# Last layer of a graph network: the gathers' schedule is set to end earlier, and the last bias is added to rows of x one step sooner

## The chip, the cores and the metric

The kernel runs on one core of one Trainium2 chip. The metric is the device time of one execution in microseconds (us), the median of several runs. Less is better.

## The reference

A graph network with 6250 nodes of 256 features, 100000 edges (src, dst; sorted by dst) and four layers:

```python
h = jnp.maximum(_layernorm(x, axis=-1), 0.0)
# three layers:
h = h + segment_sum(h[src], dst)          # each node: itself and its neighbours
h = relu(h @ W1 + b1); h = relu(h @ W2 + b2); h = h @ W3 + b3      # all 256 wide
# fourth and last layer:
h = h + segment_sum(h[src], dst)
h = relu(h @ cW1 + cb1)                   # 256 -> 256
h = relu(h @ cW2 + cb2)                   # 256 -> 64
out = x + (h @ cW3 + cb3)                 # 64 -> 256, and x is added
```

## The kernel before, in words

The nodes lie in 49 blocks of 128. 25 of them are taken as they come ("u"), and 24 hold the other nodes sorted by their number of edges ("s"). Each layer's W1 is multiplied in ahead, so that a layer begins with the neighbour sums, adds b1, and goes on with W2 and W3.

**The neighbour sums are made in two ways, side by side.** (1) *By product*: a matrix of edge counts, one byte each, lies in DRAM (`mat`). A panel is four destination blocks. For each of the 49 source blocks the bytes come to the chip (`at`), ACT or DVE turns them into numbers that TensorE reads (`a`, L1913 on ACT, L1915 on DVE, every fourth one), and TensorE does four products of 128x512 into `agg` (L1942). One source block is called a **step** here: four products. The last layer has 8 panels, 392 steps. (2) *By gather*: for 17 of the sorted blocks, POOL issues indirect DMAs, each of which fetches one neighbour row for all 128 nodes of a block (`rows`, L1627). 251 of them belong to the last layer. ACT copies the first pair of a block into `sums` (L1659), DVE adds the others (L1663), then the block's own rows (`u`, L1676 and L1677), and TensorE turns `u` (`pt`, L1690). The gathered blocks come in groups of four; the last, block 0, stands alone.

**After the sums**, panels and gathered groups take the same road. In the last layer: `head_second` (L1436, the product with cW2, into `ps`), relu on ACT (L1444), `head_third` (L1482, the product with cW3), and an addition of x to the result (`zz`, L1497, on DVE). Rows of x (`xt`) are loaded by `head_rows` when `head_second` is issued: "u" blocks by SP's queue, "s" blocks by an indirect DMA of POOL (L1459). cb3 (`row`) is added to `xt` on DVE when `head_third` is issued (L1476). Results of "s" blocks leave by indirect DMAs on POOL (L596), others by SP's queue. The last panel and block 0 are in a hurry: their x came long before (`ask_first`), and their last addition is L1502. There are three buffers for `zz`, two of PSUM for `ps`, eleven pairs of `rows`, and four for `xt`.

**What sets the order.** All this is written out by a planner while the program is built. A step counts `now` up by one; a clock in estimated us grows with every product. `later(n, f)` writes f's instructions n steps on, and `job` and `queue` do so in a span of steps. For a layer's gathers `begin` sets a pace: from nine units after the layer before has been stored to `CLOSE` (2) units ahead of the layer's end, in equal parts. `flow` and `send` write the gathers by this pace, and each is made to wait for the product that stood last in the program when it was written; `advance` writes the additions and turns of `pair`, `whole` and `finish` by the same pace. A group's W2 and W3 steps follow its turn by fixed distances (`far`, 7 steps; 5 for the last group of four). Each engine takes its own instructions strictly in the order written.

Of the kernel before, what the change touches and what calls it, by code (L numbers as in the profile page):

```python
# [16 lines left out]
OP = mybir.AluOpType  # L17
PSUM = bass.MemoryType.PSUM
DRAM = bass.MemoryType.DRAM
P = 128  # L20
# [400 lines left out]
def sorted_edges(  # L421
# [39 lines left out]
    nc = tc.nc  # L461
    N, C = x.shape
    (E,) = src.shape
    NLAYER = W1s.shape[0]
# [32 lines left out]
    early = [(0, 3)] + [(b, 4) for b in range(3, 27, 4)] + [(27, 3)]  # L497
# [58 lines left out]
    def rows_io(ap, t0, n, sb, load):  # L556

        whole = n if t0 + n < NT or LAST == P else n - 1
        got = []
        if whole:  # L560
            d = ap[t0 * P:(t0 + whole) * P, :].rearrange("(t p) c -> p t c", p=P)
            s = sb[:, :whole, :]
            got.append(nc.sync.dma_start(out=s if load else d, in_=d if load else s))
        if whole < n:
            for r0, r1 in ((0, LAST // 16 * 16), (LAST // 16 * 16, LAST)):
                d = ap[(t0 + whole) * P + r0:(t0 + whole) * P + r1, :]
                s = sb[r0:r1, whole, :]
                got.append(nc.sync.dma_start(out=s if load else d, in_=d if load else s))
        return got
# [12 lines left out]
    def wrote(key, ins, scattered=False):  # L582

        for name, alone in written.setdefault(key, []):
            if scattered or alone:
                tc.declare_no_dep(ins.ins, name, reason="each row is written once")
        written[key].append((ins.ins.name, scattered))
# [3 lines left out]
    def place_rows(key, ap, b, sb):  # L591

        if placing[0]:
            nc.gpsimd.memset(mark, 0.0)
        placing[0] = True
        got = nc.gpsimd.indirect_dma_start(  # L596
            out=ap, out_offset=bass.IndirectOffsetOnAxis(ap=ids[:, b:b + 1], axis=0),
            in_=sb, in_offset=None)
        wrote(key, got, True)
# [72 lines left out]
    def after(ins, reason, what=None):  # L672

        what = paced if what is None else what
        if what:
            tc.add_manual_dep(
                ins.ins, what[0],
                mybir.DependencyInfo(mybir.DependencyClass.Sync,
                                     mybir.DependencyReason.DATA),
                reason=reason,  # L680
            )
# [419 lines left out]
    with tc.manual_schedule():  # L1101
# [52 lines left out]
        weights = {}  # L1154
# [144 lines left out]
        due, jobs, now, free = [], [], [0], [0]  # L1299

        def later(n, fn):
            due.append((now[0] + n, fn))
# [5 lines left out]
        queue = []  # L1308
# [92 lines left out]
        def mlp(l, blocks, h1, hurry, far):  # L1401
# [5 lines left out]
            h2, xts = [], []  # L1407
            key = f"table{l + 1}"

            def runs_of(i, m):  # L1410

                part = [(i + q, 1, *blocks[i + q]) for q in range(m)]
                if m == 2 and part[0][2] == "u" and part[1][2:] == ("u", part[0][3] + 1):
                    return [(i, 2, "u", part[0][3])]
                return part
# [34 lines left out]
            def head_rows():  # L1450
                if hurry:
                    return
                for o, f, m in ((0, 0, front), (NOUT, front, n - front)):
                    if not m:
                        continue
                    xt = late.tile([P, 2, C], F32, name="xt", bufs=4)
                    for i, k, kind, b in runs_of(f, m):
                        if kind == "s":
                            got = nc.gpsimd.indirect_dma_start(  # L1459
                                out=xt[:, i - f, :], out_offset=None, in_=x[:, :],  # L1460
                                in_offset=bass.IndirectOffsetOnAxis(ap=ids[:, b:b + 1], axis=0))
                            after(got, "rows are asked for evenly over a layer")
                        else:
                            if b + k == NT and LAST < P:
                                nc.vector.memset(xt[:, i - f + k - 1, :], 0.0)
                            rows_io(x, b, k, xt[:, i - f:i - f + k, :], True)
                    xts.append(xt)

            def head_third():
                w3, row = weights[l][1]  # L1470
                sets = [(o, f, m) for o, f, m in ((0, 0, front), (NOUT, front, n - front)) if m]
                pss = []
                for k, (o, f, m) in enumerate(sets):
                    if not hurry:
                        xt = xts[k]
                        nc.vector.tensor_tensor(xt[:, :m, :], xt[:, :m, :],  # L1476
                                                row[:, None, :].to_broadcast([P, m, C]), OP.add)
                    pss.append(ps_m.tile([P, W], F32, name="ps"))
                for q in range(front):
                    for (o, f, m), ps in zip(sets, pss):  # L1480
                        if q < m:
                            mm = nc.tensor.matmul(ps[:, q * C:(q + 1) * C],  # L1482
                                                  h2[0][o:o + NOUT, 0, q * P:(q + 1) * P],
                                                  w3[o:o + NOUT, :], start=True, stop=True)
                    passed(C * FULL32, mm)

                def give(f, m, z):
                    for i, k, kind, b in runs_of(f, m):
                        if kind == "s":
                            place_rows("out", out[:, :], b, z[:, i - f, :])  # L1490
                        else:
                            for got in rows_io(out, b, k, z[:, i - f:i - f + k, :], False):
                                wrote("out", got)

                def ended(f, m, ps, z, xt):
                    if not hurry:
                        nc.vector.tensor_tensor(z[:, :m, :],  # L1497
                                                ps[:, :m * C].rearrange("p (q c) -> p q c", c=C),
                                                xt[:, :m, :], OP.add)
                        return  # L1500
                    for q in range(m):
                        nc.vector.tensor_tensor(z[:, q, :], ps[:, q * C:(q + 1) * C],  # L1502
                                                first_x[blocks[f + q]][:, 0, :], OP.add)

                for k, ((o, f, m), ps) in enumerate(zip(sets, pss)):
                    z = work.tile([P, 2, C], F32, name="zz", bufs=3)
                    xt = None if hurry else xts[k]
                    later(soon, lambda f=f, m=m, ps=ps, z=z, xt=xt: ended(f, m, ps, z, xt))
                    later(soon + 1, lambda f=f, m=m, z=z: give(f, m, z))
# [56 lines left out]
            def thirds():  # L1566
                passed(BURST)
                if end:
                    head_third()
                    return  # L1570
                for i in range(0, n, 2):
                    third(i)

            wait = 1 if hurry else far - 2
            queue.append(dict(steps=[seconds, thirds], first=now[0] + wait,
                              last=now[0] + wait + (0 if hurry else SPAN),
                              far=2 if hurry else far, hurry=hurry))


        class ByNode:  # L1580
# [21 lines left out]

            def begin(self):
                self.first = clock[0] + LAG
                self.pace = (begun[self.l] + work_of(self.l) - CLOSE - self.first) / len(self.order)

            def flow(self):
                if self.first is not None:
# [254 lines left out]
        last = [len(panels[l]) - 1 for l in range(NLAYER + 1)]  # L1863
        units = [(0, -1, j) for j in range(PRE)] + [
            (l, p, j) for l in range(NLAYER + 1) for p in range(last[l] + 1) for j in range(NT)]
        LAG, CLOSE = 9.0, 2.0
        COLS, FULL32, TURN, BUILD, SLOW, BURST = 0.457e-3, 1.68e-3, 0.4, 0.25, 1.0, 0.3
        clock = [0.0]
        FAR, SPAN = 7, 6
# [5 lines left out]
        def work_of(l):  # L1875

            t = sum(n for _, n in panels[l]) * P * NT * 2 * KC * COLS
            t += len(layers[l].blocks) * TURN
            for k, n in ((l, NT - panels[l][-1][1]), (l - 1, panels[l - 1][-1][1])):
                t += (k >= 0) * n * (P * KC + C) / 2 * (1 if k == NLAYER else 4) * FULL32  # L1880
            t += 2 * (len(nodes_of[l]) + last[l]) * BURST
            if l == 0:
                t += BUILD * UNITS * BUILT + PRE * (SLOW - BUILD)
            return t

        def passed(t, ins=None):

            clock[0] += t
            if ins is not None:
                paced[:] = [ins.ins.name]  # L1890
                for g in layers:
                    g.flow()
# [85 lines left out]
        with tc.tile_pool(name="hots", bufs=1) as hots, tc.tile_pool(  # L1978
# [6 lines left out]
            begun = {0: clock[0]}  # L1985
# [94 lines left out]
```

## Time and profile before

| | |
|---|---|
| runs | 2000.32, 2002.68, 2003.56 us; median 2002.68 us |
| the profiled execution | 1999.98 us, its span 1998.2 us |
| granted TensorE clock, mean | 0.976 |
| last layer's 392 steps | the last products end at 1981.5 us of the span |
| from there to the end of the span | 16.7 us |

Times in the rows are us from the start of the span. A row of the timeline gives start, duration, engine, line, operation and count, and in brackets how long the engine stood idle before it and what released it. The chain of waits is followed back from the last instruction; its rows give start, duration and what ran. In the view by stretches each engine has its busy time and, in brackets, its number of instructions; PEclk is the granted clock of TensorE, 1.00 being full speed.

### The profile page before, as it was taken

What the parts mean: (1) busy time and instruction counts of PE and PEld (TensorE: products, weight loads), DVE (VectorE), ACT (ScalarE), POOL (GpSimd) and SP (SyncE); (2) the same over time, 40 slices, a digit from 0 to 9 for tenths busy, and PEclk for the clock granted to TensorE, in tenths of its full rate; (3) what the DMA queues carried; (4) which work ended last, traced back from release to release, by engine and by line L of the source; (5) the groups of instructions that cost most, each with busy time, mean ns of one, the idle gap of its engine ahead of it and who ended that gap; (6) DMA issues with size and microseconds to landing.
All of it is one profiled execution on the core that took longest, in us unless ns stands there. A gap on an engine that the chain in (4) does not pass through costs nothing.

```text
span 1998.2 us, 29053 instructions
## 1 busy us (share of the span) xinstructions
PE 1883.4 (94%) x9236; PEld 1471.0 (74%) x9236; DVE 1030.9 (52%) x2211; ACT 1075.0 (54%) x2166; POOL 1309.6 (66%) x1447
## 2 busy tenths in 40 slices
PE   5856999999999899999999999999999999999997
PEld 3744777777777777777789777777788777777765
DVE  7887887676756343333335443433345354343433
ACT  4745776676767564444445464444445564454442
POOL 2526766766666556777777476676777366777775
PEclk9876999999999999999999999999999999999998
DMA  5524656666656575565557575564657476665653
GB/s 167 177 75 141 202 182 191 199 199 200 208 171 215 160 233 162 173 183 168 181 179 210 160 247 175 154 194 146 196 165 236 147 217 200 186 197 175 181 175 109
DMA packets 252334, 361.40 MB, mean 181 GB/s; under 512 B 33353, under 2 KB 206313, under 8 KB 252155
## 3 DMA queue, kind: packets, MB, share of 16 engines
q1 hardware_dynamic: 188160, 190.34, 30.2%
q0 software_dynamic: 61952, 166.87, 28.0%
q10 hardware_dynamic: 2058, 2.25, 0.4%
q8 instruction: 74, 1.21, 0.2%
q14 instruction: 90, 0.73, 0.1%
HBM read 292.33 MB, written 67.40 MB: 180 GB/s over the span
## 4 chain that ended last, share of the span: by engine, by line
PE 82%; DVE 7%; DMA 5%; issue 3%; POOL 2%; ACT 1%; SPq 0%; DVEq 0%; ACTq 0%; POOLq 0%
PE agg L1942 64%; PE ps L1519 6%; PE ps L1422 6%; DMA rows<-table,idxN 3%; PE bp L1259 2%; PE bp L1050 1%; DVE ws L768 1%; DVE hi L1205 1%; POOL rows L1627 1%; PE pt L1690 1%; POOL lane L1748 1%; DVE lo L1205 1%; PE ps L1436 1%; PE ps L1482 0%; ACT a L1913 0%
## 5 line engine op out<-in xcount | busy, mean ns | idle before, releaser
L1942 PE MATMUL agg<-a,XY 128*128 128x512 f32 (+1 forms) x6272 | 1508.8, 392 | 16.0 <-DVE a L1915 7.3
L1627 POOL DMA_INDIRECT rows<-table,idxN x1121 | 1084.5, 967 | 474.6 <-PE agg L1942 202.6
L1942 PEld LDWEIGHTS agg<-a,XY 128*128 128x128 f32 x6272 | 1142.6, 189 | 249.5 <-issue 12.4
L1913 ACT CAST a<-at 128x512 fp32r<-128x512 uint8 (+1 forms) x1249 | 707.3, 601 | 235.0 <-PE agg L1942 225.7
L1663 DVE TENSOR_TENSOR sums<-sums,rows 128x512 f32<-128x512 f32 x477 | 331.7, 695 | 502.2 <-DMA rows<-table,idxN 461.3
L1915 DVE CAST a<-at 128x512 fp32r<-128x512 uint8 (+1 forms) x312 | 142.0, 460 | 166.3 <-PE agg L1942 143.3
L1267 ACT CAST at<-bp 128x392 uint16<-128x392 f32 x227 | 110.0, 488 | 127.2 <-PE bp L1259 122.0
L1422 PE MATMUL ps<-h,w 128*128 128x512 f32 (+2 forms) x336 | 135.0, 545 | 0.3 <-DVE zz L1524 0.3
L1519 PE MATMUL ps<-w,h 128*128 128x256 f32 x588 | 133.9, 379 | 0.0
L1205 DVE TENSOR_TENSOR lo<-lanes,pairs 128x512 bf16<-128x512 bf16 x256 | 106.7, 422 | 45.6 <-PE bp L1259 44.9
L1259 PEld LDWEIGHTS <-lo 128*128 128x128 bf16 x1028 | 57.0, 102 | 97.3 <-DVE lo L1205 41.4
L1259 PE MATMUL bp<-hi,lo 128*128 128x98 bf16 x1028 | 94.4, 218 | 34.5 <-DVE lo L1205 27.7
L1519 PEld LDWEIGHTS ps<-w,h 128*128 128x128 f32 x588 | 111.5, 190 | 16.0
L596 POOL DMA_INDIRECT table<-zz,ids x72 | 72.5, 1007 | 68.3 <-DVE zz L1524 49.3
L1659 ACT COPY sums<-rows 128x512 f32<-128x512 f32 x74 | 43.8, 592 | 126.4 <-DMA rows<-table,idxN 91.2
L1425 ACT ACTIVATE h<-ps,bias 128x512 f32<-128x512 f32 (+2 forms) x84 | 51.6, 636 | 96.2 <-PE ps L1422 96.1
L1422 PEld LDWEIGHTS ps<-h,w 128*128 128x128 f32 x336 | 62.9, 192 | 52.8 <-issue 37.6
L1698 ACT ACTIVATE h<-pt,bias 128x256 f32<-128x256 f32 (+1 forms) x84 | 33.0, 444 | 127.7 <-PE pt L1690 127.7
L1524 DVE TENSOR_TENSOR zz<-ps,w 128x512 f32<-128x512 f32 (+1 forms) x81 | 50.5, 638 | 96.6 <-PE ps L1519 83.2
L1349 DVE TENSOR_TENSOR XY<-back,XY 128x256 fp32r<-128x256 f32 x138 | 54.7, 422 | 46.3 <-ACT XY L1348 45.9
L1956 ACT ACTIVATE h<-agg,bias 128x512 f32<-128x512 f32 (+1 forms) x60 | 37.3, 669 | 72.5 <-PE agg L1942 72.3
L1205 DVE TENSOR_TENSOR hi<-hi,pairs 128x784 bf16<-128x784 bf16 x128 | 72.7, 568 | 4.4
(239 smaller groups left out, 957.3 us busy)
## 6 DMA issues: line engine op xcount, KB each, us to landing
at<-mat SPq DMA_DIRECT2D x140, 448.0 KB
mat<-at SPq DMA_DIRECT2D x32, 784.0 KB
at<-mat SPq DMA_DIRECT2D x62, 336.0 KB
rows<-table,idxN POOLq DMA_INDIRECT x1121
back<-table SPq DMA_DIRECT2D x138, 128.0 KB
table<-zz SPq DMA_DIRECT2D x35, 256.0 KB
at<-mat SPq DMA_DIRECT2D x63, 112.0 KB
own<-zz SPq DMA_DIRECT2D x55, 128.0 KB
```

The source lines that it names most:

```text
L596: got = nc.gpsimd.indirect_dma_start(out=ap, out_offset=bass.IndirectOffsetOnAxis(ap=ids[:, b:b + 1], axis=0), in_=sb, in_offset=None)
L1205: nc.vector.tensor_tensor(o, values, which[:, :, None, :].to_broadcast(shape), op)
L1259: mm = nc.tensor.matmul(bp[:, m * HW:(m + 1) * HW], lo[:, m, :], hi[:, m, :], start=(i == 0), stop=(i == len(sets) - 1))
L1267: nc.scalar.copy(o, v)
L1349: later(1, lambda: nc.vector.tensor_tensor(XY[:, j:j + m, C:], z[:, :m, :], XY[:, j:j + m, :C].bitcast(F32), OP.subtract))
L1422: mm = nc.tensor.matmul(ps[:, :w], weights[l][0][:, c, i * P:(i + 1) * P], h1[:, c, :w], start=(c == 0), stop=(c == KC - 1))
L1519: mm = nc.tensor.matmul(o, h2[0][:, c, nodes], w3[:, c, :], start=(c == 0), stop=(c == KC - 1))
L1627: got = nc.gpsimd.indirect_dma_start(out=t[:, c % 2, :], out_offset=None, in_=tables[self.l][:, :], in_offset=bass.IndirectOffsetOnAxis(ap ...
L1663: nc.vector.tensor_tensor(sums, sums, rows.rearrange("p h c -> p (h c)"), OP.add)
L1913: nc.scalar.copy(o, v)
L1915: nc.vector.tensor_copy(o, v)
L1942: mm = nc.tensor.matmul(agg[c][:, :w], XY[:, j, o:o + P], a[:, :w], start=(i == 0 and half == 0), stop=(i == NT - 1 and half == 1))
```

## The change

Two things change, both in the last layer.

1. In `begin`, the last layer's gathers are laid out to end `4 * CLOSE` (8) units ahead of the layer's end, where it was `CLOSE` (2). The other layers keep 2. The additions and turns that use the gathered rows are written by the same pace and move with them.
2. The addition of cb3 to `xt` leaves `head_third`. It is written by `later(far - 1, ...)` when the rows are asked for, so one step ahead of `head_third`, which comes `far` steps after. What is computed is the same.

```diff
                     xts.append(xt)
+                    later(far - 1, lambda xt=xt, m=m: nc.vector.tensor_tensor(
+                        xt[:, :m, :], xt[:, :m, :],
+                        weights[l][1][1][:, None, :].to_broadcast([P, m, C]), OP.add))
...
             def head_third():
-                w3, row = weights[l][1]
+                w3 = weights[l][1][0]
...
-                for k, (o, f, m) in enumerate(sets):
-                    if not hurry:
-                        xt = xts[k]
-                        nc.vector.tensor_tensor(xt[:, :m, :], xt[:, :m, :],
-                                                row[:, None, :].to_broadcast([P, m, C]), OP.add)
+                for _ in sets:
                     pss.append(ps_m.tile([P, W], F32, name="ps"))
...
             def begin(self):
                 self.first = clock[0] + LAG
-                self.pace = (begun[self.l] + work_of(self.l) - CLOSE - self.first) / len(self.order)
+                early = 4 * CLOSE if self.l == NLAYER else CLOSE
+                self.pace = (begun[self.l] + work_of(self.l) - early - self.first) / len(self.order)
```

The changed file is shorter by one line above the third product, so L1482, L1497 and L1502 read L1481, L1496 and L1501 in it; the bias addition L1476 reads L1468.

**TensorE, about 160 steps from the end of the layer.** `ps` at L1436 is the second product of a gathered group, `agg` the panels' products, `pt` a turn. Before:

```order
L1482 MATMUL ps<-cw_15930,h_17693 128x256 x4
L1942 MATMUL agg<-a,XY 128x512 x32
L1690 MATMUL pt<-ident,u 128x128 x2
L1942 MATMUL agg<-a,XY 128x512 x44
L1436 MATMUL ps<-h_17461,w_15928 64x256 x4
```

and now:

```order
L1481 MATMUL ps<-cw_15930,h_17697 128x256 x4
L1942 MATMUL agg<-a,XY 128x512 x16
L1690 MATMUL pt<-ident,u 128x128 x2
L1942 MATMUL agg<-a,XY 128x512 x44
L1436 MATMUL ps<-h_17439,w_15928 64x256 x4
```

The third product (first row) belongs to a panel and stands at the same step in both, 173 steps ahead of the layer's end. The second product of the gathered group follows 76 products later before and 60 now: 154 and 158 steps ahead of the end, so it moved four steps. Its four gathers of x on POOL moved with it.

**TensorE, the end of the layer.** The `pt` in the first row shown is block 0's, the last one; L1436 of 64x128 and L1482 (now L1481) without a count are block 0's two products, and the last L1436 and L1482 are the last panel's. Before:

```order
L1690 MATMUL pt<-ident,u 128x128 x2
L1942 MATMUL agg<-a,XY 128x512 x12
L1482 MATMUL ps<-cw_15930,h_19340 128x256 x4
L1436 MATMUL ps<-h_19361,w_15928 64x128 x2
L1482 MATMUL ps<-cw_15930,h_19398 128x256
L1436 MATMUL ps<-h_19376,w_15928 64x256 x4
L1482 MATMUL ps<-cw_15930,h_19409 128x256 x4
```

and now:

```order
L1690 MATMUL pt<-ident,u 128x128 x2
L1436 MATMUL ps<-h_18901,w_15928 64x256 x4
L1942 MATMUL agg<-a,XY 128x512 x20
L1481 MATMUL ps<-cw_15930,h_19319 128x256 x4
L1942 MATMUL agg<-a,XY 128x512 x16
L1436 MATMUL ps<-h_19310,w_15928 64x128 x2
L1942 MATMUL agg<-a,XY 128x512 x4
L1481 MATMUL ps<-cw_15930,h_19391 128x256
L1436 MATMUL ps<-h_19399,w_15928 64x256 x4
L1481 MATMUL ps<-cw_15930,h_19409 128x256 x4
```

Block 0's turn stood 12 products (3 steps) ahead of the layer's end and stands 40 (10 steps) ahead now. Behind it and ahead of the end there are now also the last group's second product (L1436, four instructions, which stood ahead of the turn before), its third product (L1481) and block 0's second product, which both came after the last `agg` before.

**DVE, the end of the layer.** `h` at L1953 is half of the last panel's relu, `u` the sums of block 0. Before:

```order
L1677 TENSOR_TENSOR u<-u,sums 128x256
L1953 TENSOR_SCALAR h_19376<-agg,bias 128x512
L1476 TENSOR_TENSOR xt<-xt,cb3r 128x512 x2
L1497 TENSOR_TENSOR zz<-ps,xt 128x512 x2
L1502 TENSOR_TENSOR zz<-ps,back 128x256 x5
```

and now:

```order
L1677 TENSOR_TENSOR u<-u,sums 128x256
L1915 CAST a<-at 128x512
L1468 TENSOR_TENSOR xt<-xt,cb3r 128x512 x2
L1915 CAST a<-at 128x512
L1496 TENSOR_TENSOR zz<-ps,xt 128x512 x2
L1953 TENSOR_SCALAR h_19399<-agg,bias 128x512
L1501 TENSOR_TENSOR zz<-ps,back 128x256 x5
```

The last group's bias additions and its additions of x stood behind the last panel's relu and stand ahead of it now, with casts for the product still to come between them.

More of the change, by code (lines that the diff above doesn't have):

```diff
@@ L1574, in mlp @@
             wait = 1 if hurry else far - 2
-            queue.append(dict(steps=[seconds, thirds], first=now[0] + wait,
-                              last=now[0] + wait + (0 if hurry else SPAN),
-                              far=2 if hurry else far, hurry=hurry))
+            queue.append(dict(
+                steps=[seconds, thirds], first=now[0] + wait,
+                last=now[0] + wait + (0 if hurry else SPAN), far=2 if hurry else far, hurry=hurry))
         class ByNode:
```

## The prediction

> **What bounds the kernel now.** I read the page first, then the chain of waits over the last 120 us, then the timelines of POOL and TensorE there.
>
> ```profile
> PE 1883.4 (94%) x9236; PEld 1471.0 (74%) x9236; DVE 1030.9 (52%) x2211; ACT 1075.0 (54%) x2166; POOL 1309.6 (66%) x1447
> 1717.00:1790.00 73.00, 55.36 (x61) 1.00 0.63 193
> 1790.00:1811.50 21.50, 14.23 (x15) 1.00 0.62 187
> 1811.50:1974.70 163.20, 125.17 (x139) 0.99 0.56 168
> L1627 POOL DMA_INDIRECT rows<-table,idxN x99 | 95.7, 967 | 30.7 <-issue 15.8 <-PE agg L1942 10.9 <-DVE sums L1663 0.9
> 1810.66 0.94 POOL L1627 DMA_INDIRECT rows<-table,idxN  x1 [0.89 <-PE agg L1942]
> 1811.91 0.95 POOL L1459 DMA_INDIRECT xt<-in_x_dram,ids  x1 [0.30 <-PE ps L1436]
> 1973.66 0.94 POOL L1627 DMA_INDIRECT rows<-table,idxN  x1 [0.31 <-issue]
> ```
>
> TensorE is busy for 94% of the span, so over the whole it is the bound. The next three rows are stretches, POOL's busy time behind the length. An indirect DMA costs POOL 0.95 to 0.97 us and a pause of 0.30 even where it waits for nothing, so POOL is full at 0.76 busy. It is full from 1717 to 1790 (55.4 of 73), is not from 1790 to 1811 (14.2 of 21.5), and is full again from 1811 to the last gather at 1973.66 (125.2 of 163.2). The fifth row says the same of the 99 gathers from 1811 on: 30.7 us of idle time ahead of them, 0.31 each. At 1810.66 a gather still waited for TensorE; after it none really did. In the last 160 us POOL is behind, and its own rate decides when rows come.
>
> ```profile
> 1973.66 2.79 DMA rows<-table,idxN
> 1976.58 0.71 DVE sums L1663
> 1977.76 0.43 DVE u L1677
> 1978.33 0.41 PE pt L1690 x2
> 1978.74 2.79 PE agg L1942 x12
> 1982.30 1.29 DVE xt L1476 x2
> 1983.63 0.56 DVE zz L1497
> 1988.36 2.63 DMA out_dram<-zz,ids
> 1991.73 0.41 DVE zz L1502 x2
> ```
>
> The end of the chain of waits (rows of it). The last gather lands, its sums are done, block 0 is turned at 1978.33: 4.67 us from the issue. Twelve products end the layer at 1981.53. I call this point P. Then the bias additions (1.29 us), the additions of x, four scatters of POOL, the landing of the fourth at 1990.99, and the last additions, done at 1992.14. The stores and the end of the program take the 6.06 us to 1998.2.
>
> ```profile
> 1919.39 3.06 PE L1942 MATMUL agg<-a,XY 128*128 128x512 f32 x12 [1.55 <-DVE a L1915]
> 1924.54 2.01 PE L1942 MATMUL agg<-a,XY 128*128 128x512 f32 x4 [2.08 <-ACT a L1913]
> 1978.33 0.41 PE L1690 MATMUL pt<-ident,u 128*128 128x128 f32 x2 [1.38 <-DVE u L1677]
> 1925.50:1926.50 1.00, 1.00 (x4) 0.50 0.47 131
> 1927.50:1928.50 1.00, 1.00 (x4) 0.72 0.54 164
> 1928.50:1930.00 1.50, 1.50 (x8) 1.00 0.87 204
> ```
>
> TensorE stands still for 1.55, 2.08 and 1.38 us in the last panel, each time for gathered rows: directly, or because a cast stands in DVE's or ACT's queue behind an addition that waits for them. After the second wait the granted clock was near half from 1924.5 to 1928.2, as the last three rows show. At half rate 3.7 us cost 1.8 us.
>
> **The change part by part.** No instruction is added or removed: the same gathers, x rows, scatters and SP loads stand in other places.
>
> *When do the gathers end?* The new pace spreads six planner units over 251 gathers. Where POOL waits for TensorE, a gather moves by as many steps as its place in the program; where POOL is full, nothing moves it but the work ahead of it. The full stretch that reaches the end begins with the four gathers of x at 1811.91, which wait for the second product 154 steps ahead of the end. That product now stands at 158. The queue ahead has room: between 1790 and 1811 POOL was idle beyond its pauses by 21.5 - 14.23/0.76 = 2.8 us, and the earlier pace lets it begin that stretch sooner. So POOL starts its last run four steps sooner. It then works off the same instructions, so the last gather is issued four steps sooner.
>
> ```profile
> 1903.52 10.27 PE agg L1942 x44
> 1900.21 1.01 PE ps L1436 x8
> 1913.79 1.06 PE ps L1482 x8
> 1903.30 0.22 PE pt L1690 x2
> ```
>
> Eleven steps take 10.27 us, so a step is 0.934 us, and four are 3.74 us. Bounds: 2.8 us (only the slack between 1790 and 1811) and 5.6 us (all six steps). I take 3.7, since it follows from the place in the program.
>
> *What waits for it?* Block 0's turn moved seven steps, from 3 to 10 ahead of the end, while its last row comes only four steps sooner. So this wait grows. The turn cannot start ahead of 1978.33 - 3.74 = 1974.59. TensorE is there long before: it reached the old place at 1978.33 - 1.38 = 1976.95, and seven steps (6.5) and the last group's second product (1.01) lie behind the turn now, so it would come at 1969.4, plus what the waits in the middle change. The wait at the turn is some 5 us. **This is the step on which the forecast rests.** It also covers whatever else the change does to TensorE in the middle of the panel, up to 5 us either way.
>
> *From the turn to P.* The turn 0.22, the second product 1.01, ten steps 9.34, the third product 1.06, and block 0's second product about 0.31 (half of the row of 0.62 below, which ran slowly): 11.94 us. P would be 1986.5 where it was 1981.53: +5.0. (A trace row counts each fp32 matmul twice: x8 is four instructions.)
>
> *The clock.* 2.08 us of waiting were enough to halve it, so some 5 us are. Cost 1.8 us, as in the row. Bounds: 0 and 3.6 (twice the span). The half rate after the earlier waits was paid before too, and is covered by the wait anyway. +1.8.
>
> *From P to the last addition.*
>
> ```profile
> 1981.16 0.69 ACT L1956 ACTIVATE h<-agg,bias 128x512 f32<-128x512 f32 x1 [1.76 <-PE agg L1942]
> 1984.99 0.36 ACT L1444 ACTIVATE h<-ps,bias 64x128 f32<-64x128 f32 x1 [3.14 <-PE ps L1436]
> 1984.33 0.62 PE L1436 MATMUL ps<-h,w 128*64 128x128 f32 x4 [1.75 <-DVE zz L1497]
> 1985.40 0.70 PE L1482 MATMUL ps<-cw,h 64*128 64x256 f32 x2 [0.45 <-ACT h L1444]
> 1986.03 1.97 PE L1436 MATMUL ps<-h,w 128*64 128x256 f32 x8
> 1988.10 0.47 ACT L1444 ACTIVATE h<-ps,bias 128x256 f32<-128x256 f32 x1 [2.75 <-PE ps L1436]
> 1988.63 2.08 PE L1482 MATMUL ps<-cw,h 64*128 64x256 f32 x8 [0.63 <-ACT h L1444]
> 1990.73 1.42 DVE L1502 TENSOR_TENSOR zz<-ps,back 128x256 f32<-128x256 f32 x4 [4.17 <-PE ps L1482]
> ```
>
> It took 10.6 us, for bias, additions and scatters of the last group stood in it. They stand ahead of P now. What is left, by these rows: ACT's relu ends 0.3 behind P (1981.16 + 0.69); block 0's relu 0.36 and a handover to P + 0.8; its third product and the start of the next, 0.63, to P + 1.4; the second product of the last panel at full clock 1.01, to P + 2.4; relu with handovers 0.63, to P + 3.1; the third product at full clock, of which three quarters are needed for the first addition, 0.9, to P + 4.0; four additions 1.42, to P + 5.4. So 5.2 us are saved. But these two products took 1.97 and 2.08 us before, not 1.01 and 1.06, because the clock had fallen after a gap of 1.75 and one of 0.45 us. The new gaps are a little shorter. I take one of the two products at half rate, +1.0; bounds 0 and +2.0.
>
> [...]
>
> *The bias one step sooner.* 22 additions of x rows move by a step. In the last group this is part of the 5.2. Elsewhere it makes DVE stand for x rows if POOL brings them late, with row additions and casts queued behind. Priced at nothing: what it does to TensorE lies ahead of the turn, under its 5 us.
>
> *Sum.* +5.0 + 1.8 - 5.2 + 1.0 = **+2.6 us** on the profiled 1999.98, and as much on the median of 2002.68: **2005.3 us**. The profiled execution is 2.7 below the median, so runs differ by more than this sum. Bounds: with no clock lost -0.2; with all of it lost +5.4; with the gathers' shift at 2.8 a further +0.9, at 5.6 a further -1.9.
>
> **The rivals.** About 0.2%, 4 us, is what a measurement of this kernel can tell from no change.
>
> *The clock holds* in the tail, or at the turn too: +1.6 or -0.2, 2002.5 to 2004.3. For it: 1.38 us at 1978.33 brought no fall. Against: 1.75 did.
>
> *POOL is held up by DVE, slower.* The place: the middle of the last panel. DVE stands at the bias addition for x rows that POOL has not yet fetched; it frees no row buffers meanwhile; POOL, out of pairs, stops; and every us that it stops is one at the last gather, uncovered. It decides once DVE stands longer than eleven pairs last, 22 gathers at 1.25 us less those under way. Against: of the gathers' idle time only 0.9 us is put down to DVE before. With 4 us lost: +6.6, 2009.3.
>
> *The waits go away, faster.* If rows came in time, the waits of 1.55, 2.08, 1.38 and the 1.8 of clock would go: P at 1981.53 - 6.8 + 1.4 (products moved ahead of it) = 1976.1, the last addition 5.4 later at 1981.5 instead of 1992.1: -10.6, 1992.1. Half of it gives 1997.4. For it: this is the stretch where TensorE waits. Against: POOL has no free slot in the last 160 us.
>
> **How the numbers follow.** The forecast, a longer wait at the last turn paid back by a shorter tail, has 45%, with a range of its own from 2003 to 2008; 15 of these points are above +4 (both tail products slow, a longer fall of the clock). The clock holds: 13%. Slower by POOL: 24%. Faster: 18%. Within 0.2%: 30 + 13 = 43%. Slower: 24 + 15 = 39%. Faster: 18%. The range that leaves two in ten out goes from 1998 to 2010.
>
> **What would show it.** Right: the last gather 3 to 5 us sooner against the start of the last layer; a wait of 4 to 6 us ahead of block 0's turn, with a clock near 0.5 behind it; P some 5 to 7 us later; about 6 us instead of 10.6 from P to the last addition, with no scatter in the chain. Wrong: a wait under 2 us at the turn, POOL idle for TensorE or DVE after 1811, or the last gather no sooner.

## The result and the profile after

| | before | after |
|---|---|---|
| median of 22 runs each, on one chip | 2000.74 us | 2004.94 us |
| ratio after/before | | 1.0013, 95% interval 1.0007 to 1.0019 |
| span of the profiled execution | 1998.2 us | 2003.1 us |
| granted TensorE clock, mean | 0.976 | 0.977 |

By the ratio the change costs 2.6 us (1.4 to 3.8). The medians lie 4.2 us apart and the means of the same runs 3.1: the change is slower by all three, by how much is less sure than the interval says. The two spans differ by more, 4.9 us, but 2.7 of these lie ahead of the last layer, where the change edits nothing. So the last layer is measured from its own start, its first gather. The timeline of POOL has it, in the kernel before:

```profile
1589.38 0.97 POOL L1627 DMA_INDIRECT rows<-table,idxN  x1 [11.54 <-PE agg L1942]
```

and in the changed kernel, with the first gather of x in POOL's last run, the last gather, and the gathers' group from there on:

```profile
1592.10 0.97 POOL L1627 DMA_INDIRECT rows<-table,idxN  x1 [11.72 <-PE agg L1942]
1810.93 0.95 POOL L1459 DMA_INDIRECT xt<-in_x_dram,ids  x1 [0.30 <-PE ps L1436]
1972.47 0.98 POOL L1627 DMA_INDIRECT rows<-table,idxN  x1 [0.30 <-issue]
L1627 POOL DMA_INDIRECT rows<-table,idxN x98 | 94.3, 962 | 29.9 <-issue 14.3 <-PE agg L1942 10.4 <-DMA rows<-table,idxN 1.2
```

Against the layer's start the last gather is issued at 380.37 us; it was 384.28. So it is 3.9 us sooner, and not six steps (5.6 us, the prediction's upper bound). The last row says why: 98 gathers with 29.9 us of idle time ahead of them, 0.31 each, which is POOL's own pause. As before, POOL has nothing to give in the last 160 us; it started this stretch 3.7 us sooner (1810.93 - 1592.10 = 218.83, where it was 222.53) and ended it as much sooner.

TensorE's timeline of the changed kernel, from the middle of the last panel to the end:

```profile
1922.14 3.78 PE L1942 MATMUL agg<-a,XY 128*128 128x512 f32 x8 [5.59 <-DVE a L1915]
1977.06 0.41 PE L1690 MATMUL pt<-ident,u 128*128 128x128 f32 x2 [3.37 <-DVE u L1677]
1978.41 6.47 PE L1942 MATMUL agg<-a,XY 128*128 128x512 f32 x20
1985.88 4.00 PE L1942 MATMUL agg<-a,XY 128*128 128x512 f32 x16
1989.80 0.65 PE L1436 MATMUL ps<-h,w 128*64 128x128 f32 x4
1990.38 1.18 PE L1942 MATMUL agg<-a,XY 128*128 128x512 f32 x4
1992.14 0.70 PE L1481 MATMUL ps<-cw,h 64*128 64x256 f32 x2 [0.57 <-ACT h L1444]
1992.76 1.08 PE L1436 MATMUL ps<-h,w 128*64 128x256 f32 x8
1994.48 1.13 PE L1481 MATMUL ps<-cw,h 64*128 64x256 f32 x8 [0.63 <-ACT h L1444]
```

The waits of 1.55 and 2.08 us in the middle became one of 5.59, and the wait of 1.38 at block 0's turn became 3.37. The last products end at 1991.56 (P). The two products of the tail ran in 1.08 and 1.13 us where they took 1.97 and 2.08. The granted clock (PEclk) behind the turn, by stretches:

```profile
1978.00:1979.00 1.00, 1.00 (x7) 0.53 (x4) 0.69 (x1) 1.00 (x4) 0.67 (x1) 0.70 0.46 131
1979.00:1980.00 1.00, 1.00 (x4) 0.80 (x3) 0.00 (x0) 1.00 (x3) 0.00 (x0) 0.50 0.48 131
1980.00:1982.00 2.00, 2.00 (x7) 1.58 (x6) 1.03 (x2) 0.04 (x1) 0.00 (x0) 0.55 0.00 0
1982.00:1984.00 2.00, 2.00 (x10) 1.61 (x9) 0.00 (x0) 0.00 (x0) 0.00 (x0) 1.00 0.00 0
1991.00:1997.00 6.00, 3.41 (x21) 1.60 (x19) 2.53 (x6) 1.41 (x3) 1.88 (x3) 1.00 0.21 71
```

The shares missing to 1.00 make 0.30 + 0.50 + 0.90 = 1.7 us. The last row is the tail: 1.00 throughout. The chain of waits covers only the last 0.66 us here, with no scatter and no transfer in it (its three rows). What stands ahead of it is in DVE's timeline (last row): the last four additions waited for the third product.

```profile
1996.40 0.20 DVE zz L1501
1996.60 0.05 issue
1996.65 0.41 DVE zz L1501
1995.64 1.42 DVE L1501 TENSOR_TENSOR zz<-ps,back 128x256 f32<-128x256 f32 x4 [2.35 <-PE ps L1481]
```

The last addition ends at 1997.06, 404.96 us after the layer's start, where it was 402.77: **2.2 us later**, near the 2.6 of the ratio. The rest of the span is 6.04 us, where it was 6.05.

### The profile page after: what moved, and what is told of

It reads as the page before. It is cut to its first block, busy times and chain, and to the rows that moved or that the text cites. A ratio compares the mean times of both kernels' runs of the same rounds, so it can differ in the third digit from the quotient of the medians.

```text
span 2003.1 us, 29042 instructions
## 1 busy us (share of the span) xinstructions
PE 1882.5 (94%) x9236; PEld 1470.6 (73%) x9236; DVE 1031.9 (52%) x2211; ACT 1074.8 (54%) x2166; POOL 1311.6 (65%) x1447
```

## The experiments

This table has, for each kernel whose trace is used, the last gather's issue and the end of the last addition in us from the layer's first gather (each against before in brackets), the time from there to the end of the span, and the time against before by the ratio, with its interval. Each kernel has one trace, and not all were taken on one chip; the ratios compare runs of one chip.

| kernel | last gather | last addition | to the end | time against before, us |
|---|---|---|---|---|
| before | 384.28 | 402.77 | 6.05 | |
| the change | 380.37 (-3.9) | 404.96 (+2.2) | 6.04 | +2.6 (+1.4 to +3.8) |
| bias alone | 384.67 (+0.4) | 403.38 (+0.6) | 5.88 | -1.6 (-3.4 to +0.2) |
| pace alone | 381.05 (-3.2) | 405.56 (+2.8) | 6.05 | +2.8 (+1.0 to +4.6) |
| change, wait filled | 380.42 (-3.9) | 403.43 (+0.7) | 5.85 | -1.0 (-2.8 to +0.8) |
| change, x rows by SP | 365.87 (-18.4) | 388.84 (-13.9) | 12.76 | -8.2 (-11.4 to -5.2) |
| bias, gathers ahead | 374.24 (-10.0) | 402.29 (-0.5) | 5.89 | -1.2 (-3.0 to +0.4) |
| the same, x rows asked early | 373.88 (-10.4) | 394.98 (-7.8) | 5.82 | -8.8 (-11.2 to -6.4) |
| the same, pace 6 units | 370.84 (-13.4) | 390.82 (-11.9) | 6.14 | -12.2 (-15.6 to -9.0) |

### The two parts apart

The bias addition moved, the pace as before:

```diff
-                early = 4 * CLOSE if self.l == NLAYER else CLOSE
+                early = CLOSE
```

> The bias part alone; the gathers' pace is that of before. Theory (the change's cost is the wait at block 0's turn, which comes from the pace): the turn stays 3 steps ahead of the end with a wait of about 1.4 us, P does not move, and the 1.29 us of bias additions leave the chain behind P: 1 to 1.5 us faster than before. Rival (the cost is DVE standing at the earlier bias addition for x rows, 6.59 and 1.73 us in the middle of the last panel of the change): slower than before by 1 to 4 us, with those waits of DVE in the trace.

The median was 2001.5 us against 2002.63, ratio 0.9992 (0.9983 to 1.0001). TensorE's timeline, and a row of DVE's:

```profile
1919.84 2.08 PE L1942 MATMUL agg<-a,XY 128*128 128x512 f32 x4 [6.26 <-DVE a L1915]
1980.30 0.41 PE L1690 MATMUL pt<-ident,u 128*128 128x128 f32 x2
1986.10 0.62 PE L1436 MATMUL ps<-h,w 128*64 128x128 f32 x4 [1.54 <-DVE zz L1496]
1988.29 1.97 PE L1436 MATMUL ps<-h,w 128*64 128x256 f32 x8
1990.89 2.08 PE L1481 MATMUL ps<-cw,h 64*128 64x256 f32 x8 [0.63 <-ACT h L1444]
1984.00 0.69 DVE L1468 TENSOR_TENSOR xt<-xt,cb3r 128x512 f32<-128x512 f32 x1 [1.85 <-DMA xt<-in_x_dram,ids]
```

The moved addition does make DVE stand in the middle of the panel: the gap there is 6.26 us. But the turn behind it then waits for nothing (1.4 us were expected), and no loss against before is shown. The last gather did not come later by more than 0.4 us. The rival in which the bias addition holds up POOL falls. The gain of 1 to 1.5 us is not shown either: the ratio's interval holds both it and nothing, and in the trace the last addition comes 0.6 us later. The last row shows why the tail (what follows P) is no shorter: the last group's bias addition still ends behind P, since it waits for x rows that POOL fetches behind the last gather.

The pace alone, with the bias addition in its old place:

```diff
-                self.pace = (begun[self.l] + work_of(self.l) - CLOSE - self.first) / len(self.order)
+                early = 4 * CLOSE if self.l == NLAYER else CLOSE
+                self.pace = (begun[self.l] + work_of(self.l) - early - self.first) / len(self.order)
```

> The pace part alone; the bias stays in the third step. Theory: block 0's turn stands 10 steps ahead of the end and waits 3 to 5 us for its rows, the clock falls to 0.5 behind it, P comes 5 to 7 us later than before against the start of the layer, the tail takes 5.5 to 6 us; 2 to 3.5 us slower than before, as the whole change. Rival (DVE at the bias addition): the gap of TensorE near 1920 shrinks from 5.6 to under 3 us and the time is that of before within 1 us.

2004.67 us against 2002.63, ratio 1.0014 (1.0005 to 1.0023): the whole cost of the change. At the end of the layer TensorE shows the same picture as the whole change, the wait longer, since the middle has shorter gaps than the change (3.02 and 1.18 us):

```profile
1919.38 4.92 PE L1943 MATMUL agg<-a,XY 128*128 128x512 f32 x20 [3.02 <-ACT a L1914]
1972.96 0.66 PE L1691 MATMUL pt<-ident,u 128*128 128x128 f32 x2 [4.08 <-DVE u L1678]
1973.55 1.98 PE L1436 MATMUL ps<-h,w 128*64 128x256 f32 x8
1990.27 1.13 PE L1482 MATMUL ps<-cw,h 64*128 64x256 f32 x8 [0.63 <-ACT h L1444]
```

The waits in the middle are no shorter than before (3.02 and 1.18 us, where 1.55 and 2.08 stood), and the turn waits 4.08 where it waited 1.38. The 3.02 us kept the clock: the 20 products behind them took 4.92 us. The tail is short and at full clock here too, so it is the pace that shortens it, by moving the last group's work ahead of P.

### The clock behind the wait

The change, with 24 transposes that nobody reads written ahead of block 0's turn, so that TensorE works while it waits:

```diff
+                    if self.l == NLAYER and b == 0:
+                        for _ in range(24):
+                            nc.tensor.transpose(self.pt[:, 0, :P], ident, ident)
```

> The change, with 24 needless transpositions of a constant (about 2.6 us of TensorE work, overwritten at once) ahead of block 0's turn, so that TensorE works instead of waiting there. Theory (1.7 us of the loss are the clock behind that wait): the clock stays at 1.00 behind the turn and 1.5 to 1.9 us are won against the change: 0.5 to 1.5 us slower than before. Rival (the clock costs nothing, or the wait is not the bound): 2.5 us slower than before as the change, or 2.6 us more, slower by 5.

2001.2 us, ratio 0.9995 (0.9986 to 1.0004). The filler, the turn, and the products behind it:

```profile
1970.37 2.78 PE L1691 MATMUL pt<-ident 128*128 128x128 f32 x24
1974.35 0.44 PE L1693 MATMUL pt<-ident,u 128*128 128x128 f32 x2 [1.20 <-DVE u L1677]
1975.73 4.93 PE L1945 MATMUL agg<-a,XY 128*128 128x512 f32 x20
```

The 20 products took 4.93 us where they took 6.47, and the last addition comes 1.5 us sooner than in the change. So the half clock after the wait costs what the windows gave, 1.5 to 1.7 us, and by the trace the kernel is 0.7 us slower than before, as expected. By the two ratios the kernel won 3.6 us on the change, with intervals of 1.2 and 1.8 us on either side; more than the profile shows, and not told apart from it.

### Fewer gathers on POOL

The change, with the x rows of sorted blocks loaded by SP's queue. They are taken as they lie in DRAM and not by the sorted list, so other rows of x are added; the bytes are the same.

```diff
-                            got = nc.gpsimd.indirect_dma_start(
-                                out=xt[:, i - f, :], out_offset=None, in_=x[:, :],
-                                in_offset=bass.IndirectOffsetOnAxis(ap=ids[:, b:b + 1], axis=0))
-                            after(got, "rows are asked for evenly over a layer")
+                            rows_io(x, b, 1, xt[:, i - f:i - f + 1, :], True)
```

> The change, with the x rows of sorted blocks loaded by SP's queue from block order instead of POOL's indirect DMAs: wrong rows of x are added there, at the same number of bytes. 18 of POOL's last 132 indirect DMAs go, 22 us of its queue. Theory (POOL's rate sets the last gather): the last gather comes 10 to 20 us sooner, the waits of TensorE in the last panel and at the turn fall under 1 us, and the kernel is 8 to 16 us faster than before. Rival (rows land in time and the waits come from the order on DVE and ACT): the last gather moves, the time stays within 2 us of the change.

1994.84 us, ratio 0.9959 (0.9943 to 0.9974). The last gather comes 18.4 us sooner than before, TensorE has no gap in the last panel, and the turn waits for nothing, though it stands 10 steps ahead of the end as in the change:

```profile
1961.98 0.41 PE L1687 MATMUL pt<-ident,u 128*128 128x128 f32 x2
```

So it is POOL's queue that made rows late. Gathered rows and rows of x both come sooner here; this kernel does not part the two. The last addition comes 13.9 us sooner, and only 8.2 us arrive in the time: the end of the program takes 12.76 us behind it instead of 6. The view of waits has in this kernel

```profile
SPq L2073 <- PEq L2073: 7.6, 2, 7.0
```

and in the changed kernel, for the same wait (us in total, times, longest):

```profile
SPq L2076 <- PEq L2076: 0.7, 2, 0.5
```

SP's queue waits 7.0 us for TensorE's sequencer at the very end, though TensorE's last product ended 14 us before the span does. What its sequencer did there the trace does not show.

### Gathers ahead, consumers in place

The next three kernels give up the change's pace and let each gather of the last layer be sent further ahead of its additions. The first has before's pace, the moved bias addition, and:

```diff
-                    self.send(int((clock[0] - self.first + LAG) / self.pace) + 1)
+                    self.send(int((clock[0] - self.first + (2 * LAG if self.l == NLAYER else LAG)) / self.pace) + 1)
```

The second also asks for the x rows of a group when the group is put in the queue, and not at its second product; the bias addition keeps its step. (In the functions of the changed kernel: `head_rows()` at the end of `mlp`, and the `later(far - 1, ...)` in `seconds`.) The third has 18 units written in place of `2 * LAG`, which is the same number since `LAG` is 9, and lays its gathers out to end `3 * CLOSE` (6 units) ahead of the layer's end: it differs from the second in this pace alone. A fourth kernel is the change with `8 * CLOSE` in place of `4 * CLOSE`.

> The change with its pace taken back (the last layer spreads its gathers over the same time as before) and, in its place, every gather of the last layer sent LAG = 9 more units of work ahead of its additions; the additions, turns and products stay where before has them. Theory (the change loses because its consumers, above all block 0's turn, move further than the last gather does): here the turn stays three steps ahead of the end, so the wait ahead of it must be no longer than the bias-alone kernel's, and the time is not above that of before: -3 to 0 us, with the tail of 5 to 6 us between the end of the products and the last addition less what cold products cost. The gap in the middle of the last panel may grow (vector engine standing at the bias addition for x rows that now queue behind nine units more of gathers), 5 to 8 us, and be covered. Rival (any earlier laying-out of the gathers costs, since POOL then collides with other work): 2 us or more above before. Rival (only the last gather's issue decides): as much faster as the last gather is sooner, 4 to 8 us.

> The change with 8 * CLOSE (16 units) in place of 4 * CLOSE (8). Theory: POOL works off the same instructions at 1.25 us each, and its last run begins with the gathers of x rows, which move with their place in the program; the last gather comes some 8 to 12 us sooner than in before, but block 0's turn moves as far again, so the time stays 1 to 4 us above that of before, and the wait at the turn stays 2 to 5 us. Rival (the plan's intent: gathers that end sooner give a shorter time): 4 us or more below before. Rival (each unit of pace costs more): 5 us or more above before.

> As the kernel that sends the last layer's gathers 9 units further ahead with before's pace and the bias addition early; and the x rows of the last layer are asked for when a group is put in the queue (ahead of its second product by some ten steps) and not at the second product itself, while the bias addition keeps its step. Theory (the waits in the last panel are consumers that come ahead of their rows: DVE at the bias addition, then block 0's turn): both go, no gap above 1.5 us in the last panel, the clock stays at 1.00 to the turn, and the time is 6 to 11 us below before. Rival (POOL's rate alone decides the end, whatever stands where): last gather as in before and within 2 us of before. Rival (the end of the program, which came 12.75 us behind the last addition and not 6.0 in the run with x rows by SP, takes a part back): 2 to 5 us below before, with the span's end 10 us or more behind the last addition.

> As the run before it, with the gathers a fixed 18 units ahead of their place and a pace of 3 * CLOSE (6 units) in the last layer. Theory: the last gather comes some 10 us sooner than in before, nothing waits for it, the last panel runs without a gap, and the time is 3 us or so below the run before it, 9 to 14 us below before. Rival (the program's end takes it back): not below the run before it, with the span's end 10 us or more behind the last addition. Rival (POOL then stands without pairs of row buffers and is held up): the last gather is no sooner than in the run before it and the time is equal or more.

These four first ran on a chip on which the kernel before takes 2176.41 us. In the order of these expectations they gave ratios of 1.0021 (1.0007 to 1.0035), 1.0031 (1.0015 to 1.0047), 1.0033 (1.0016 to 1.0049) and 1.0010 (0.9993 to 1.0027). In the groups of before, on the first chip, TensorE's main products have this idle time ahead of them over the span:

```profile
L1942 PE MATMUL agg<-a,XY 128*128 128x512 f32 (+1 forms) x6272 | 1508.8, 392 | 16.0 <-DVE a L1915 7.3 <-ACT a L1913 3.9 <-DVE a L1911 2.7
```

and in the kernel with x rows asked early, on this chip:

```profile
L1944 PE MATMUL agg<-a,XY 128*128 128x512 f32 (+1 forms) x6272 | 1572.4, 401 | 106.6 <-issue 73.6 <-ACT a L1915 15.8 <-ACT h L1958 6.8
```

"issue" is time in which the engine waited for nothing that the profile shows: 73.6 us of it, summed over the span. There TensorE often stands by itself, and the layer's end is set by that as well as by rows. So none of the expectations, which are sums of waits for rows, is decided by these ratios. Of the kernel with `8 * CLOSE` they say no more than that it isn't faster there (6.7 us above before, 3.3 to 10.2); its turn waits 2.16 us for its rows. It has no run on another chip; the other three have.

> The kernel of the first rows-ahead run once more. In that call the kernel before itself took 2176 us and TensorE's main products stood 73.6 us for nothing that the profile names, in any layer, so nothing was told apart. On a chip where before takes some 2002 us: theory (the waits in the last panel are consumers that come ahead of their rows): no gap above 1.5 us for rows in the last panel, 6 to 11 us below before. Rival (POOL's rate alone decides): within 2 us of before. Rival (the program's end takes a part back): 2 to 5 us below, with 10 us or more from the last addition to the span's end. Where before takes 2176 us again: no difference beyond the interval.

> The second rows-ahead kernel once more (18 units, 3 * CLOSE), for the same reason. Theory: last gather some 10 us sooner than in before, nothing waits for it, 9 to 14 us below before. Rival (the program's end takes it back): not below the first rows-ahead kernel. Rival (POOL stands without row buffers): last gather no sooner than in the first.

> The kernel with before's pace, the bias early and the gathers 9 units further ahead, x rows asked for as in before, once more for the same reason. Theory: its turn stays three steps ahead of the end, so -3 to 0 us against before, with a gap of 5 to 8 us in the middle of the last panel at the bias addition, for the x rows queue behind nine units more of gathers. Rival (any earlier laying-out costs): 2 us or more above before.

On a chip where before takes 2001.91 us they gave, in this order, 1993.53 us, 0.9956 (0.9944 to 0.9968); 1989.74 us, 0.9939 (0.9922 to 0.9955); and 2000.67 us, 0.9994 (0.9985 to 1.0002). The last of these, with the gathers ahead alone, comes first here:

```profile
1915.64 2.08 PE L1942 MATMUL agg<-a,XY 128*128 128x512 f32 x4 [7.46 <-DVE a L1915]
1975.52 0.38 PE L1690 MATMUL pt<-ident,u 128*128 128x128 f32 x2
1981.60 0.62 PE L1436 MATMUL ps<-h,w 128*64 128x128 f32 x4 [1.85 <-DVE zz L1496]
1911.49 0.69 DVE L1468 TENSOR_TENSOR xt<-xt,cb3r 128x512 f32<-128x512 f32 x1 [13.72 <-DMA xt<-in_x_dram,ids]
```

(TensorE's rows and one of DVE's.) Its last gather is **10.0 us sooner** than before, its turn waits for nothing, and yet its last addition is 0.5 us sooner. The gain is lost in the middle: the x rows are now behind nine units more of gathers in POOL's queue, DVE stands 13.72 us at the bias addition, its casts stand behind it, and TensorE stands 7.46 us. The tail has half rate besides, behind a gap of 1.85 us. With the x rows asked early, and the same gathers (last one at -10.4):

```profile
1901.93 1.39 DVE L1557 TENSOR_TENSOR xt<-xt,cb3r 128x512 f32<-128x512 f32 x2 [2.69 <-DMA xt<-in_x_dram,ids]
1945.04 0.69 DVE L1557 TENSOR_TENSOR xt<-xt,cb3r 128x512 f32<-128x512 f32 x1 [9.88 <-DMA xt<-in_x_dram,ids]
1947.46 4.00 PE L1944 MATMUL agg<-a,XY 128*128 128x512 f32 x16 [1.15 <-DVE a L1917]
1970.40 0.38 PE L1692 MATMUL pt<-ident,u 128*128 128x128 f32 x2
1977.06 0.62 PE L1436 MATMUL ps<-h,w 128*64 128x128 f32 x4 [2.41 <-DVE zz L1493]
1978.75 1.08 PE L1436 MATMUL ps<-h,w 128*64 128x256 f32 x8
1984.82 0.76 DVE L1498 TENSOR_TENSOR zz<-ps,back 128x256 f32<-128x256 f32 x2 [2.43 <-PEq L2054]
```

The same addition stands 2.69 us, and the time is 8.8 us below before, 7.6 below the kernel without the early x rows. DVE still stands 9.88 us at the next group's addition, near 1945, but that costs TensorE only 1.15 us, its largest gap in the last 75 us ahead of P: it seems to matter which cast is queued behind, and when TensorE needs it. The two differ in nothing but when the x rows are asked for. Not all of the 7.3 us between their last additions are waits for rows: the tail's two products kept the clock here and did not there, 1.08 and 1.14 us for 1.96 and 2.08, which is 1.8 us. On the other side the last two additions stood 2.43 us for TensorE's sequencer (last row), which no other kernel of the table did; without that the last addition would be 10.2 us sooner than before, and not 7.8.

The third, with the pace of 6 units, has its last gather at -13.4 and takes 12.2 us less than before. It was expected to run without a gap, and has one:

```profile
1947.27 3.06 PE L1944 MATMUL agg<-a,XY 128*128 128x512 f32 x12 [2.18 <-DVE a L1917]
1969.63 0.38 PE L1692 MATMUL pt<-ident,u 128*128 128x128 f32 x2
```

It beats the kernel before and the change. That it beats the second is not told apart: the intervals overlap, and of the 4.2 us between the last additions 2.43 are the sequencer's. Its pace moves additions and turns as the change's does, and block 0's turn (second row) stands 32 products, 8 steps, ahead of the end. It waits for nothing there. So an earlier pace does no harm here, where the rows are asked for far enough ahead.

### The change, with the x rows asked early

One more kernel was meant to tell what in the change itself waits: its pace and its turn, with the x rows asked early.

> The change as it is, with one part of the rows-ahead kernels alone: the x rows of the last layer are asked for when a group is put in the queue; pace, LAG and block 0's turn as in the change. Theory (the change loses at block 0's turn, which stands 10 steps ahead of the end and waits for the last gather, and POOL works through the same instructions without a pause): the gap at the bias addition in the middle of the panel shrinks or moves, but the turn is covered by the last gather all the same, with a wait of 3 to 6 us there and half the clock behind it; time -1 to +3 us against before. Rival (the change loses because DVE stands at the bias addition for x rows; with them here, nothing is lost): 6 us or more below before, as in the first rows-ahead kernel.

It ran on another chip of the slower kind (before 2180.47 us): 2178.25 us, ratio 0.9994 (0.9977 to 1.0011). TensorE waits 3.96 us for a cast 16 products ahead of the turn, and not at the turn itself, but with idle time of its own all over the span (61.0 us put to "issue" in the main products) this settles nothing, and the trace does not show the wait of 3 to 6 us at the turn that was expected. Whether the change would gain by early x rows alone is open.

## Why the prediction was right

**The last gather** was to come 3.74 us sooner, by the place of POOL's last run in the program: 3.9 measured. POOL stayed full from 1811 on.

**The wait at block 0's turn**, the step on which the forecast rested, is there: 3.37 us and not some 5, because the gaps in the middle of the panel took more of it (5.59 us, where 1.55 and 2.08 stood). The prediction had said that the wait at the turn covers what happens in the middle. The runs bear this out: with the pace alone the middle has 3.02 and 1.18 and the turn 4.08, and the turn comes 4.62 us behind the last gather's issue, 4.59 in the change. The turn itself came 3.99 us sooner against the layer's start (384.96, it was 388.95), as the last gather.

**From the turn to P**: 11.94 + 1.8 = 13.7 us were predicted, 14.5 measured. The clock's part came out, 1.7 for 1.8, but its reason (2.08 us were enough to halve the clock, so some 5 are) is no rule: with the pace alone 3.02 us kept it. The road itself was a little too cheap. By the starts of TensorE's rows, the turn took 0.34 us (0.22 predicted), the last five steps 3.92 and 1.18 (3.74 and 0.93), and block 0's second product 0.58 (0.31). The last was misread: the prediction halved the row of 0.62 before as one that ran slowly, but the granted clock was 1.00 there.

**The tail**: 5.4 us from P to the last addition were predicted at full clock, and 5.50 measured. The term for one product at half rate, +1.0, was wrong: both ran at full rate (1.08 and 1.13 us, granted clock 1.00). The prediction had read from two rows that a gap of about 2 us is followed by half rate. That is no rule either, as the runs of this study show: 1.54 us of standing in front of block 0's second product, and 0.45 behind it, lost the clock in the kernel with the bias alone (1.97 us for the last panel's second product), while 2.41 us and 0.45 at the same places kept it in the kernel with x rows asked early (1.08 us).

So the sum is -3.99 + (14.50 - 3.20) - (10.62 - 5.50) = +2.2 us in the profiled layer, by terms that were predicted as -3.74, +10.5, -5.2 and +1.0. The +1.0 that was not there and the 0.8 that the turn's road cost more nearly cancel. That the sum came so near is luck to that extent; the wait at the turn and the shorter tail are not.

**The rivals.** The clock holds: true of the tail, not of the turn. This rival's price for the tail alone, +1.6, lies within the interval too. POOL held up by DVE at the bias addition: half right. DVE does stand there, 6.59 us in the changed kernel (first row, from DVE's timeline), but POOL did not stop, and no cost of the bias alone is shown (-1.6 us, -3.4 to +0.2).

```profile
1917.12 0.69 DVE L1468 TENSOR_TENSOR xt<-xt,cb3r 128x512 f32<-128x512 f32 x1 [6.59 <-DMA xt<-in_x_dram,ids]
1919.54 0.69 DVE L1468 TENSOR_TENSOR xt<-xt,cb3r 128x512 f32<-128x512 f32 x1 [1.73 <-DMA xt<-in_x_dram,ids]
```

The waits go away, priced at -10.6: not what this change does, but what the kernels with gathers and x rows ahead do, by -8.8 and -12.2. So the price was of the right size; its condition, rows that come ahead of their consumers, is what the change does not bring about, since it moves the consumers with the gathers, and the turn of block 0 further than its rows.

## What to carry to other kernels

A schedule that ends a stream of transfers earlier gained nothing here, where it moved the consumers by the same table: with POOL's queue full, the transfers moved by what its last run began sooner (3.7 us, and 3.9 at the last gather), block 0's turn by its place in the program (seven steps), and the difference became a wait (3.37 us at the turn). Set the requests further ahead of their consumers first (with that, the earlier pace cost nothing), and look at every other consumer of the same queue: 10 us won at the last gather were lost at an addition that waited for x rows behind it. And sum the waits of a stage as one: here a later wait for the same queue covered an earlier one. With the wait at the turn gone and 7.46 us in the middle the last addition came 0.5 us sooner than before, with no gap above 1.15 us in the last 75 us ahead of P and again none at the turn it came 7.8 us sooner.

## What the runs showed of the hardware

- **Between 1.5 and 3 us the length of a gap did not decide the clock in these runs.** Gaps of 1.54, 1.75, 1.85 and 2.08 us were followed by half rate, gaps of 1.55, 2.18, 2.41 and 3.02 us were not (1.54, 1.75, 1.85 and 2.41 had 0.45 us more of idle time behind the next product). All those of 3.37 us and more shown here (3.37, 3.96, 4.08, 5.59, 6.26, 7.46) were followed by it. Half rate is a granted clock of 0.50 behind 1.54, 1.75, 1.85, 2.08, 3.37, 4.08 and 5.59 us; behind 6.26 and 7.46 four products took 2.08 us, where four took 1.18 at full rate, and behind 3.96 us sixteen took 5.55, where sixteen took 4.00. Full rate is a granted clock of 1.00 behind 1.55 and 2.41 us, 12 products in 3.06 us behind 2.18, and 20 in 4.92 behind 3.02. The one of 3.37 us brought some 3.4 us at half rate, twice the 1.7 us that it cost.
- **The end of a program can cost more.** 5.8 to 6.1 us from the last addition to the end of the span in eight kernels, 12.76 in the ninth, with a wait of 7.0 us for TensorE's sequencer. In one of the eight DVE stood 2.43 us for it ahead of the last two additions. The cause is open.
- **Chips differ in more than speed.** On two chips the kernel before takes 2176 and 2180 us where it takes 2001 to 2003 on the others, and TensorE stands without a reason that the profile shows (73.6 and 61.0 us put to "issue" in the main products of the two kernels read above). In the timeline of the kernel with `8 * CLOSE` some products start 1.40 us apart, or one and a half times as much:

```profile
2086.81 0.59 PE L1942 MATMUL agg<-a,XY 128*128 128x512 f32 x1 [0.81 <-issue]
2088.91 0.58 PE L1942 MATMUL agg<-a,XY 128*128 128x512 f32 x1 [1.51 <-issue]
2090.31 0.59 PE L1942 MATMUL agg<-a,XY 128*128 128x512 f32 x1 [0.81 <-issue]
```

  What paces them is not shown. The same kernel that is 8.8 us faster than before on one chip was 7.2 us slower (1.0033, 1.0016 to 1.0049) on one of these. A schedule tuned on one chip need not hold on another.
